# A four-layer graph kernel on one NeuronCore: all issue times of its 64 pipelined graphs laid out anew

## The chip, the cores and the metric

The kernel runs on one core of a Trainium2 chip. The core has five instruction streams that run beside each other: TensorE (PE in the profile, with its weight loads as PEld), VectorE (DVE), ScalarE (ACT), GpSimd (POOL) and SyncE (SP), which here only issues DMAs. Each stream takes its instructions strictly in the order in which the program holds them, and waits at an instruction until the inputs and the buffers of that instruction are free. The metric is the device time of one execution in microseconds; the median of several executions counts.

## The reference

64 graphs of 256 nodes with 512 features go through four layers. Every layer normalizes, applies a graph operation and adds the result to its input:

```python
# x: (64, 256, 512), adj: (64, 256, 256)
for layer in (L0, L1, L2, L3):
    h = jnp.maximum(_layernorm(x, axis=-1), 0.0)
    x = x + layer(h, adj, ...)

# L0: w = softmax_nodes(sum_m((q k^T / 8) * adj)),  out = w * (h Wv^T)
# L1: attention of 8 heads: leaky_relu(e_self + e_neigh), masked by adj, softmax, times features
# L2: per head tanh(adj * (Xc Xp^T)) Xp, with Xc = Xp C^T
# L3: w = softmax_nodes(sum_d(q * (adj k)) / sqrt(512)),  out = w * (h Wv)
```

The four layers of a graph depend on each other; the 64 graphs don't.

## The kernel before

**One graph is a list of 150 steps.** The function `graph(b)` builds them as closures under short names. A step issues a few instructions of one engine, or the DMAs of one move. By layer, with the lines of the profile:

- Every layer k begins with the same front: `st`k (row statistics, DVE, L690), `rs`k (DVE, L697), `pw`k (a power on POOL, L701), `sh`k (DVE, L706), `hn`k (the normalized rows, ACT, L713), `sq`k (a transpose of 32x32 blocks, DVE, L645), `sw`k (the blocks to DRAM, one DMA of 512 KB, L733), `ht`k (read back as turned rows, four DMAs of 128 KB, L650). The matmuls that need turned rows wait for `ht`k.
- Layer 0: `qk`, `qe`, `score0`, `s0v` (DVE, L829), `pv00`, `pv01` (values, L639), `softp0`, `softv0` (L756), `softa0`, `softw0` (L768, L769), `add0` (DVE, L775).
- Layer 1: `fa`, `fb` (features, L639), `fae`, `fbe` (DVE, L854, L855, L865), `send`, `er`, `enes` (two rows per head through DRAM and to all partitions, L873 to L884), `max0` to `max3` (DVE, L896), `mxv`, `mxt`, `mr`, `mb` (the row maxima by the same way, L906 to L926), and for each pair of heads p `ea`p (ACT, L935), `eg`p (POOL, L942), `eb`p (DVE, L948), `ex`p (ACT, L954), `po`p (PE, L966), `eh`p (POOL, L975); `su`, `oe`, `se`, `sp`, `sr`; `sqo`, `swo`, `or` (the way through DRAM again: L783, L733, L796), `oa0`, `oa1` (POOL, L1032, L1034).
- Layer 2: `xp`, `xe` (L639, L1052), `sqx`, `swx`, `xpt` (L645, L733, L650), `xc`, `ps`, `tv` (DVE, L1129), `ta`, `py`, `ye` (ACT, L1120), `sqy`, `swy`, `yr` (L783, L733, L796), and the sum with the input in two halves: `yv` (DVE, L1149) and `yg` (POOL, L1149).
- Layer 3: `am`, `agg`, `ga`, `z` (L639), `zv` (L1189), `softp3` to `softw3`, `pv30`, `pv31`, `add3`, `store`.

**The order is written out by hand, as times.** The table `TIMES` gives every step of a graph a time after the graph's beginning; graph b begins at b times `PERIOD`. `Plan.sequence` sorts all steps of all 64 graphs by these times, and `Plan.run` issues them in this order, with a dependency that keeps each engine's instructions in it. The times themselves reach the chip in no other way: only the order that they give to each engine counts. With a table of 283 us and a period of 59, about five graphs are under way at once. The first six graphs, the last five and the loads of the weights have tables of their own (`FIRST`, `LAST`, `WEIGHTS`).

**Buffers** are taken from a pool when a step is traced, the one that was given back longest ago first: 8 PSUM banks, 5 of `xt`, 4 of `pair`, 3 of `ht`, 3 of `all`, 2 each of `hn`, `sq`, `cols`, `half` and others. A step that takes a buffer waits for the last user of that buffer.

All DMAs are issued by SP, 20 steps per graph, in the one order. A step such as `ht1` waits on SP until its `sw1` has landed, and all DMAs behind it in SP's order wait too.

Of the kernel before, what the change touches and what calls it, by code (L numbers as in the profile page):

```python
# [18 lines left out]
KC = D // P  # L19
# [16 lines left out]
PERIOD = 59.0  # L36
TIMES = {
    "load": 0.000, "st0": 8.598, "at": 14.291, "rs0": 17.770, "pw0": 18.151, "sh0": 19.827, "hn0": 20.197,
    "sq0": 22.027, "neg": 23.076, "sw0": 23.619, "ht0": 26.810, "negt": 33.560, "qk0": 36.920, "qk1": 37.838,
    "qe0": 38.562, "qe1": 39.097, "score0": 39.117, "s0v": 42.489, "softp0": 45.404, "softv0": 48.091,  # L40
    "softa0": 48.731, "pv00": 49.189, "softw0": 52.829, "pv01": 53.476, "add0": 56.587, "st1": 58.282,
    "rs1": 60.040, "pw1": 60.420, "sh1": 61.401, "hn1": 61.771, "sq1": 63.601, "sw1": 65.193, "ht1": 68.384,
    "fa1": 73.209, "fa0": 75.198, "fae0": 77.504, "fae1": 78.257, "send": 79.376, "er": 79.818, "enes": 83.628,
    "max0": 93.041, "ea0": 93.130, "ea1": 95.760, "max2": 97.616, "fb0": 97.757, "max1": 97.783, "max3": 99.552,
    "mxv": 102.131, "mxt": 103.746, "ea2": 104.173, "mr": 104.189, "eg1": 105.093, "mb": 107.595, "ea3": 108.549,
    "eg0": 108.704, "eb0": 112.651, "eb1": 113.945, "ex0": 114.332, "eg2": 115.240, "ex1": 115.461, "eh1": 117.705,
    "fb1": 118.902, "fbe0": 119.237, "eg3": 120.587, "fbe1": 121.996, "po0": 122.625, "po1": 123.961,
    "eb2": 124.009, "ex2": 125.487, "eb3": 125.789, "eh0": 126.598, "ex3": 126.782, "po2": 127.022, "oe0": 127.910,
    "su0": 128.127, "po3": 128.638, "eh3": 128.740, "oe1": 129.974, "eh2": 130.055, "sqo": 130.841, "su1": 131.698,
    "se": 132.525, "swo": 132.976, "or": 132.996, "sp": 136.188, "sr": 138.013, "oa0": 139.860, "oa1": 142.480,  # L50
    "st2": 145.314, "rs2": 147.072, "pw2": 147.452, "sh2": 148.433, "hn2": 148.803, "sq2": 150.633, "sw2": 152.225,
    "ht2": 155.416, "xp0": 159.864, "xp1": 163.649, "xe0": 166.754, "xe1": 167.673, "sqx": 168.592, "swx": 171.012,
    "xpt": 174.204, "xc": 179.698, "xcv": 181.830, "ps0": 183.981, "tv0": 187.172, "xca": 187.563, "ps1": 188.658,
    "ta0": 189.627, "tv3": 192.016, "tv1": 193.393, "tv2": 197.635, "ta1": 198.812, "ta3": 200.645, "ta2": 201.909,
    "py0": 202.513, "ye0": 202.533, "py1": 204.554, "ye1": 206.911, "sqy": 207.777, "swy": 211.577, "am": 212.932,
    "yr": 217.212, "yv": 221.001, "yg": 221.746, "st3": 223.517, "rs3": 225.557, "pw3": 225.938, "sh3": 230.347,
    "hn3": 230.717, "agg1": 233.270, "agg0": 235.086, "sq3": 238.587, "sw3": 240.179, "ga0": 241.452,
    "ga1": 242.287, "ht3": 248.180, "z0": 254.433, "z1": 257.973, "zv0": 258.289, "zv1": 261.830,
    "softp3": 265.594, "pv31": 265.839, "softv3": 268.089, "softa3": 268.742, "pv30": 269.380, "softw3": 274.098,
    "add3": 280.909, "store": 282.605,  # L60
# [3 lines left out]
    "wn0": 288.300, "w12": 288.700, "mt0": 289.000, "wa": 289.100, "mv0": 289.200, "sa2": 289.300, "w11": 289.400,  # L64
    "wqk": 289.500, "w10": 289.900, "sa0": 290.600, "sa1": 290.700, "wv0": 290.800, "mk": 291.000, "b1": 291.500,
    "wn1": 291.600, "w20": 292.600, "w22": 292.800, "w13": 293.200, "b2": 294.000, "mm0": 294.100, "wn2": 294.200,
    "mt1": 294.300, "mv1": 294.400, "mkp": 294.500, "mt2": 294.600, "sa3": 295.000, "mm1": 295.300, "wn3": 295.700,
    "mv2": 295.800, "w21": 296.100, "mm2": 296.300, "mt3": 298.000, "mv3": 298.200, "mm3": 298.700, "mkv": 298.800,
    "c2": 298.900, "wv3": 299.200, "w23": 301.000, "ma": 302.600, "room": 303.100,
# [367 lines left out]
def tile_four_gnn_layers(ctx: ExitStack, tc: tile.TileContext, x, adj, nodemask,  # L437
# [6 lines left out]
    nc = tc.nc  # L444
# [790 lines left out]
```

## Time and profile before

| | |
|---|---|
| time before, median of 5 runs | 3896.66 us (3888.99 to 3902.02) |
| the profiled execution: device time | 3896.66 us |
| its span, first to last instruction | 3894.9 us |
| DVE busy | 3055.0 us (78%), 7449 instructions |
| ACT busy | 1872.2 us (48%), 3653 instructions |
| POOL busy | 1531.3 us (39%), 1229 instructions |
| DMA | 784.71 MB, mean 201 GB/s |
| granted TensorE clock, mean | 0.990 |
| SP's longest kind of wait: L650 for `sq_d` to land | 485.2 us, 247 times |

The profiled execution took exactly the median's time. A busy share is an average over the whole span. What the kernel repeats is a round: in every round each engine does each of the 150 steps once, for five different graphs. So the profile is read by the round: from a step of one graph to the same step of the next.

### The profile page before, as it was taken

The page shows a single profiled execution, that of the slowest core. Times are in us where ns is not written, and L with a number is a line of the kernel's source. Part 1 is how long each engine was busy: PE and PEld are TensorE (multiplying, and loading weights), DVE is VectorE, ACT ScalarE, POOL GpSimd, SP SyncE. Part 2 cuts the span into 40 slices and gives each one's busy share as a digit, 9 for nine tenths or more (in the row PEclk, how much of TensorE's full clock was granted, in tenths as well). Part 3 has the DMA queues.
Part 4 walks back from the last instruction along what each step waited for, and adds up shares of the span by engine and source line. Part 5 has one row for each costly group of instructions (what it writes and reads, how often), then busy time and mean ns, then how long its engine had stood idle before and what let it go on. Part 6 is the DMA issues. An engine that isn't in the chain of part 4 may idle for free.

```text
span 3894.9 us, 52870 instructions
## 1 busy us (share of the span) xinstructions
PE 3680.3 (94%) x16322; PEld 2126.9 (55%) x16322; DVE 3055.0 (78%) x7449; ACT 1872.2 (48%) x3653; POOL 1531.3 (39%) x1229
## 2 busy tenths in 40 slices
PE   6789999999999999999999999999999999999889
PEld 4445555555555555555555555555555555555544
DVE  5778788888788788788787788787788788787784
ACT  2444545544544545444544545544544544554442
POOL 1434344344344344344344344344344344343341
PEclk9899999999999999999999999999999999999999
DMA  7565666666666666666666666666666666666553
GB/s 199 168 201 190 203 200 212 218 197 217 211 206 215 206 212 208 202 208 208 206 195 214 207 197 214 215 199 216 206 201 216 211 196 216 210 197 198 184 176 103
DMA packets 967435, 784.71 MB, mean 201 GB/s; under 512 B 788913, under 2 KB 859121, under 8 KB 942577
## 3 DMA queue, kind: packets, MB, share of 16 engines
q1 hardware_dynamic: 967152, 781.34, 63.9%
q8 instruction: 130, 2.13, 0.2%
q14 instruction: 153, 1.25, 0.1%
HBM read 511.12 MB, written 270.01 MB: 201 GB/s over the span
## 4 chain that ended last, share of the span: by engine, by line
PE 48%; DVE 19%; DMA 17%; SPq 8%; issue 5%; POOL 2%; ACT 1%; DVEq 0%; ACTq 0%; POOLq 0%
PE bank L639 35%; DVE sq L645 7%; DMA ht<-sq_d 6%; DMA sq_d<-sq 5%; SPq L650 5%; PE bank L1111 5%; PE bank L966 2%; DVE pair L948 2%; PE bank L1097 2%; DMA blocks<-in_adj_dram 2%; DMA hn<-sq_d 2%; DVE stats L690 2%; DVE shift L706 1%; DVE xt L775 1%; DVE junk L896 1%
## 5 line engine op out<-in xcount | busy, mean ns | idle before, releaser
L639 PE MATMUL bank<-w_s,ht 128*128 128x256 f32 (+2 forms) x3072 | 968.9, 463 | 86.2 <-DMA ht<-sq_d 76.1
L639 PE MATMUL bank<-wv_s,ht 128*128 128x512 f32 x2048 | 907.5, 595 | 0.0
L639 PEld LDWEIGHTS bank<-w_s,ht 128*128 128x128 f32 x3072 | 588.9, 198 | 388.6 <-issue 295.3
L713 ACT ACTIVATE hn<-xt,shift,rstd 128x512 f32<-128x512 f32 x512 | 388.7, 807 | 830.5 <-DVE shift L706 772.5
L942 POOL TENSOR_TENSOR pair<-pair,negt 128x1024 f32<-128x1024 f32 x256 | 603.0, 2367 | 112.7 <-ACT pair L935 112.7
L639 PEld LDWEIGHTS bank<-wv_s,ht 128*128 128x128 f32 x2048 | 397.6, 197 | 445.9 <-issue 443.7
L975 POOL TENSOR_TENSOR half<-pair 128x512 f32<-128x512 f32 x256 | 330.8, 1304 | 594.7 <-PE bank L989 326.8
L896 DVE CUSTOM_DVE_ANT_0 junk<-all,adj 128x256 f32<-128x256 f32 x1024 | 467.3, 456 | 31.4 <-issue 0.2
L639 PE MATMUL bank<-m_s,ht 128*128 128x512 f32 x1024 | 454.3, 595 | 8.3 <-DMA ht<-sq_d 6.6
L935 ACT ACTIVATE pair<-all,ec 128x256 f32<-128x256 f32 x1024 | 433.4, 497 | 10.5 <-DMA all<-er_d 10.4
L1149 POOL TENSOR_TENSOR xt<-xt,hn 128x512 f32<-128x512 f32 x64 | 111.9, 1749 | 816.2 <-DMA hn<-sq_d 816.2
L690 DVE BATCH_NORM_STATS2 stats<-xt 128x6 f32<-128x512 f32 x512 | 332.5, 682 | 92.5 <-POOL xt L1034 84.8
L701 POOL TENSOR_TENSOR rstd<-rstd,power 128x2 f32<-128x2 f32 x256 | 180.5, 705 | 406.6 <-DVE rstd L697 390.9
L645 DVE STREAM_TRANSPOSE sq<-hn 128x512 f32<-128x512 f32 x512 | 332.1, 687 | 5.1 <-ACT hn L713 4.9
L1129 DVE TENSOR_TENSOR pair<-bank,at 128x512 f32<-128x512 f32 x512 | 317.3, 670 | 12.3 <-PE bank L1097 12.1
L966 PE MATMUL bank<-pair,feats 128*64 128x256 f32 x2048 | 270.9, 399 | 59.2 <-ACT pair L954 58.6
L954 ACT ACTIVATE pair<-pair 128x1024 f32<-128x1024 f32 x256 | 264.0, 1050 | 118.3 <-DVE pair L948 111.3
L639 PEld LDWEIGHTS bank<-m_s,ht 128*128 128x128 f32 x1024 | 196.9, 197 | 220.6 <-issue 215.1
L948 DVE TENSOR_TENSOR pair<-pair,all 128x1024 f32<-128x1024 f32 x256 | 303.1, 1222 | 16.1 <-DMA all<-m_d 16.0
L1032 POOL TENSOR_TENSOR hn<-hn,rs 128x256 f32<-128x256 f32 x256 | 152.1, 616 | 393.3 <-DMA hn<-sq_d 280.5
L761 ACT ACTIVATE bank<-bank,nmax 128x256 f32<-128x256 f32 x128 | 56.9, 444 | 501.7 <-DVE nmax L756 501.7
L1136 ACT ACTIVATE pair<-pair 128x512 f32<-128x512 f32 x512 | 285.8, 617 | 16.5 <-DVE pair L1129 16.4
(83 smaller groups left out, 4545.0 us busy)
## 6 DMA issues: line engine op xcount, KB each, us to landing
sq_d<-sq SPq DMA_DIRECT2D x448, 512.0 KB
ht<-sq_d SPq DMA_DIRECT2D x1024, 128.0 KB
all<-er_d SPq DMA_DIRECT2D x128, 1024.0 KB
all<-m_d SPq DMA_DIRECT2D x64, 1024.0 KB
hn<-sq_d SPq DMA_DIRECT2D x512, 128.0 KB
xt<-in_x_dram SPq DMA_DIRECT2D x64, 512.0 KB
xpt<-sq_d SPq DMA_DIRECT2D x256, 128.0 KB
out_dram<-xt SPq DMA_DIRECT2D x64, 512.0 KB
```

Of the source, the lines that this page charges most:

```text
L639: nc.tensor.matmul(p, chunk(ht[:, k], c), w[:, k], start=(k == 0), stop=(k == KC - 1))
L645: nc.vector.transpose(sq.rearrange("p (r k i c) -> p c k r i", r=4, k=KC, c=NC)[:, c], t[:, c])
L690: nc.vector.bn_stats(stats[:, c, :], g["xt"][:, c, :])
L713: nc.scalar.activation(hn[:, c, :], g["xt"][:, c, :], AF.Relu, bias=st["shift"][:, c:c + 1], scale=st["rstd"][:, c:c + 1])
L896: nc.vector.tensor_tensor_reduce(junk, g["en"][:, h, :], g["adj"][:, c, :], 1.0, -BIG, OP.add, OP.max, g["mx"][:, c, h:h + 1])
L935: nc.scalar.activation(e[:, s, j, :], g["es"][:, h, :], AF.Prelu, bias=st["ec"][:, j, H + h:H + h + 1], alpha=0.2)
L942: nc.gpsimd.tensor_tensor(e, e, g["negt"][:, None].to_broadcast([P, 2, NC, N]), OP.add)
L948: nc.vector.tensor_tensor(e, e, g["m"][:, 2 * p:2 * p + 2, None, :].to_broadcast([P, 2, NC, N]), OP.subtract)
L966: nc.tensor.matmul(po[s * U:(s + 1) * U, p % 2, :], feats[:, j, h * U:(h + 1) * U], e[:, s, j, :], start=(j == 0), stop=(j == NC - 1))
L975: nc.gpsimd.tensor_tensor(g.take("half", name=f"h{p}"), e[:, :, 0, :], e[:, :, 1, :], OP.add)
L1129: nc.vector.tensor_tensor(th[:, s], g[f"ps{p}{s}"].rearrange("p (m n) -> p m n", m=NC), g["at"], OP.mult)
L1136: nc.scalar.activation(g[f"th{p}"][:, s], g[f"th{p}"][:, s], AF.Tanh)
```

## The change

`PERIOD`, `TIMES`, `WEIGHTS`, `FIRST` and `LAST` get new values. The steps, their instructions, their buffers and the way in which the order is issued stay. In the setup, the two banks of each of the four weight transposes get names of their own (`wt0` becomes `wt00` to `wt03`), so that the transposes of one part can stand in the order before the copies of the part before it.

```diff
-PERIOD = 59.0
+PERIOD = 57.0
 TIMES = {
-    "load": 0.000, "st0": 8.598, "at": 14.291, "rs0": 17.770, "pw0": 18.151, "sh0": 19.827, "hn0": 20.197,
-    "sq0": 22.027, "neg": 23.076, "sw0": 23.619, "ht0": 26.810, "negt": 33.560, "qk0": 36.920, "qk1": 37.838,
-    "qe0": 38.562, "qe1": 39.097, "score0": 39.117, "s0v": 42.489, "softp0": 45.404, "softv0": 48.091,
-    "softa0": 48.731, "pv00": 49.189, "softw0": 52.829, "pv01": 53.476, "add0": 56.587, "st1": 58.282,
-    "rs1": 60.040, "pw1": 60.420, "sh1": 61.401, "hn1": 61.771, "sq1": 63.601, "sw1": 65.193, "ht1": 68.384,
-    "fa1": 73.209, "fa0": 75.198, "fae0": 77.504, "fae1": 78.257, "send": 79.376, "er": 79.818, "enes": 83.628,
-    "max0": 93.041, "ea0": 93.130, "ea1": 95.760, "max2": 97.616, "fb0": 97.757, "max1": 97.783, "max3": 99.552,
-    "mxv": 102.131, "mxt": 103.746, "ea2": 104.173, "mr": 104.189, "eg1": 105.093, "mb": 107.595, "ea3": 108.549,
-    "eg0": 108.704, "eb0": 112.651, "eb1": 113.945, "ex0": 114.332, "eg2": 115.240, "ex1": 115.461, "eh1": 117.705,
-    "fb1": 118.902, "fbe0": 119.237, "eg3": 120.587, "fbe1": 121.996, "po0": 122.625, "po1": 123.961,
-    "eb2": 124.009, "ex2": 125.487, "eb3": 125.789, "eh0": 126.598, "ex3": 126.782, "po2": 127.022, "oe0": 127.910,
-    "su0": 128.127, "po3": 128.638, "eh3": 128.740, "oe1": 129.974, "eh2": 130.055, "sqo": 130.841, "su1": 131.698,
-    "se": 132.525, "swo": 132.976, "or": 132.996, "sp": 136.188, "sr": 138.013, "oa0": 139.860, "oa1": 142.480,
-    "st2": 145.314, "rs2": 147.072, "pw2": 147.452, "sh2": 148.433, "hn2": 148.803, "sq2": 150.633, "sw2": 152.225,
-    "ht2": 155.416, "xp0": 159.864, "xp1": 163.649, "xe0": 166.754, "xe1": 167.673, "sqx": 168.592, "swx": 171.012,
-    "xpt": 174.204, "xc": 179.698, "xcv": 181.830, "ps0": 183.981, "tv0": 187.172, "xca": 187.563, "ps1": 188.658,
-    "ta0": 189.627, "tv3": 192.016, "tv1": 193.393, "tv2": 197.635, "ta1": 198.812, "ta3": 200.645, "ta2": 201.909,
-    "py0": 202.513, "ye0": 202.533, "py1": 204.554, "ye1": 206.911, "sqy": 207.777, "swy": 211.577, "am": 212.932,
-    "yr": 217.212, "yv": 221.001, "yg": 221.746, "st3": 223.517, "rs3": 225.557, "pw3": 225.938, "sh3": 230.347,
-    "hn3": 230.717, "agg1": 233.270, "agg0": 235.086, "sq3": 238.587, "sw3": 240.179, "ga0": 241.452,
-    "ga1": 242.287, "ht3": 248.180, "z0": 254.433, "z1": 257.973, "zv0": 258.289, "zv1": 261.830,
-    "softp3": 265.594, "pv31": 265.839, "softv3": 268.089, "softa3": 268.742, "pv30": 269.380, "softw3": 274.098,
-    "add3": 280.909, "store": 282.605,
+    "load": 0.000, "st0": 0.020, "at": 0.040, "rs0": 0.041, "pw0": 1.190, "sh0": 5.411, "hn0": 9.143, "neg": 9.823,
+    "sq0": 13.810, "sw0": 13.830, "negt": 20.103, "ht0": 20.147, "qk1": 25.359, "qk0": 25.505, "qe0": 25.525,
+    "qe1": 31.036, "score0": 31.056, "pv00": 31.112, "s0v": 32.547, "softp0": 32.567, "softv0": 34.836,
+    "softa0": 34.856, "softw0": 35.790, "pv01": 40.387, "add0": 43.272, "st1": 43.292, "rs1": 44.358,
+    "pw1": 46.056, "sh1": 46.076, "hn1": 49.648, "sq1": 51.260, "sw1": 58.135, "ht1": 60.945, "fa0": 60.965,
+    "fa1": 62.580, "fae0": 69.453, "fae1": 70.533, "send": 70.553, "er": 70.573, "enes": 71.911, "ea0": 77.990,
+    "max0": 78.143, "ea2": 80.895, "max3": 81.818, "max1": 83.190, "fb0": 85.227, "max2": 87.498, "mxv": 87.518,
+    "mxt": 87.571, "eg0": 94.088, "mr": 94.796, "fbe0": 95.764, "ea1": 97.749, "eg1": 97.769, "mb": 98.261,
+    "fb1": 99.101, "eb0": 100.193, "eg2": 100.883, "ea3": 101.474, "ex0": 101.699, "fbe1": 102.120, "eb2": 103.469,
+    "po0": 105.075, "eg3": 106.212, "ex2": 106.927, "eb1": 108.590, "eb3": 108.607, "ex1": 108.610, "ex3": 108.627,
+    "eh1": 108.630, "po2": 110.140, "eh0": 110.672, "po1": 111.849, "po3": 112.568, "oe0": 112.800, "oe1": 112.820,
+    "su0": 113.279, "eh2": 114.993, "sqo": 115.048, "swo": 119.512, "eh3": 121.483, "su1": 121.503, "or": 123.062,
+    "se": 124.801, "sp": 126.234, "sr": 128.731, "oa0": 128.751, "oa1": 133.174, "st2": 133.194, "rs2": 133.214,
+    "pw2": 133.973, "sh2": 134.814, "hn2": 134.834, "sq2": 138.696, "sw2": 138.716, "ht2": 150.552, "xp0": 152.412,
+    "xp1": 153.173, "xe0": 156.059, "xe1": 156.636, "sqx": 156.656, "swx": 160.517, "xpt": 163.712, "xc": 163.798,
+    "xcv": 169.374, "ps0": 170.351, "tv1": 172.876, "ta1": 172.896, "xca": 176.954, "tv0": 177.175, "ps1": 182.074,
+    "ta0": 184.632, "py0": 184.652, "tv2": 186.879, "ta2": 186.899, "tv3": 187.157, "am": 187.177, "ta3": 189.350,
+    "ye0": 190.185, "py1": 191.616, "ye1": 191.636, "sqy": 191.656, "swy": 191.676, "yr": 195.931, "yg": 201.775,
+    "yv": 203.676, "st3": 204.853, "rs3": 205.841, "pw3": 205.861, "sh3": 206.511, "hn3": 209.985, "agg0": 213.022,
+    "sq3": 213.434, "sw3": 214.903, "ga0": 217.074, "agg1": 217.232, "ht3": 218.661, "z0": 220.014, "ga1": 228.472,
+    "zv0": 240.578, "z1": 240.673, "zv1": 244.494, "softp3": 244.514, "softv3": 244.534, "pv30": 249.208,
+    "pv31": 250.464, "softa3": 253.023, "softw3": 256.850, "add3": 262.864, "store": 272.661,
 }
...
@@ -594,7 +592,7 @@
             @step(f"mt{e}")
             def _():
                 for s in range(2):
-                    pt = g.take("bank", name=f"wt{s}")
+                    pt = g.take("bank", name=f"wt{s}{e}")
                     for k in range(KC):
                         nc.tensor.transpose(pt[:, k * P:(k + 1) * P], st[f"wn{e}"][:, s, k], ident)
 
@@ -602,10 +600,10 @@
             def _():
                 st["w_t"] = w_t = once.tile([P, 2, D], F32, name="w_t", bufs=1)
                 nc.vector.tensor_copy(w_t[:, 0, :].rearrange("p (k d r) -> p k d r", k=KC, r=4),
-                                      g["wt0"].rearrange("p (k r d) -> p k d r", k=KC, r=4))
-                nc.vector.tensor_copy(w_t[:, 1, :], g["wt1"])
-                g.done("wt0")
-                g.done("wt1")
+                                      g[f"wt0{e}"].rearrange("p (k r d) -> p k d r", k=KC, r=4))
+                nc.vector.tensor_copy(w_t[:, 1, :], g[f"wt1{e}"])
+                g.done(f"wt0{e}")
+                g.done(f"wt1{e}")
 
             @step(f"mm{e}")
             def _():
```

The tables `WEIGHTS`, `FIRST` and `LAST`, left out here, are replaced in the same way. At the start, the loads of graphs 0 and 1 now both stand ahead of the first weights on SP (before: that of graph 0 alone), and graph 1's steps come earlier among those of graphs 0 and 2.

What the table of the repeating round means for each engine, from the first `fa` on, follows from sorting it. The number behind a step says how many rounds earlier its graph was loaded; `-1` is the next graph:

```
before
PE: fa1.1 fa0.1 sp.2 z0.4 z1.4 py0.3 py1.3 softp3.4 pv31.4 pv30.4 qk0.0 qk1.0 fb0.1 score0.0 xp0.2 softp0.0 xp1.2
  pv00.0 pv01.0 agg1.3 agg0.3 fb1.1 xc.2 po0.1 po1.1 ps0.2 po2.1 su0.1 po3.1 ps1.2 su1.1
DVE: fae0.1 fae1.1 sh0.0 sr.2 send.1 tv2.3 sq0.0 zv0.4 zv1.4 st2.2 rs2.2 sh2.2 sqy.3 softv3.4 sq2.2 max0.1 softw3.4
  max2.1 max1.1 max3.1 s0v.0 mxv.1 yv.3 mxt.1 add3.4 st3.3 softv0.0 rs3.3 xe0.2 xe1.2 sqx.2 softw0.0 sh3.3 eb0.1 eb1.1
  add0.0 st1.0 rs1.0 fbe0.1 sh1.0 sq3.3 fbe1.1 sq1.0 eb2.1 eb3.1 st0.-1 tv0.2 sqo.1 at.-1 tv3.2 tv1.2 rs0.-1
SP: swo.2 or.2 er.1 sw0.0 enes.1 ht0.0 sw2.2 swy.3 ht2.2 yr.3 mr.1 store.4 mb.1 swx.2 xpt.2 load.-1 sw3.3 sw1.0 ht1.0
  ht3.3
POOL: oa0.2 oa1.2 pw2.2 yg.3 eg1.1 pw3.3 eg0.1 eg2.1 eh1.1 pw1.0 eg3.1 eh0.1 eh3.1 eh2.1 pw0.-1
ACT: hn0.0 ta1.3 neg.0 ta3.3 ta2.3 ye0.3 ye1.3 hn2.2 softa3.4 negt.0 ea0.1 am.3 ea1.1 qe0.0 qe1.0 ea2.1 softa0.0 ea3.1
  hn3.3 ex0.1 ex1.1 hn1.0 xcv.2 ga0.3 ga1.3 ex2.1 ex3.1 oe0.1 xca.2 oe1.1 ta0.2 se.1
after
PE: fa0.1 fa1.1 su1.2 ps1.3 sp.2 z1.4 py0.3 softp3.4 py1.3 pv30.4 pv31.4 qk1.0 qk0.0 fb0.1 score0.0 pv00.0 softp0.0
  xp0.2 xp1.2 pv01.0 agg0.3 fb1.1 agg1.3 po0.1 z0.3 xc.2 po2.1 po1.1 po3.1 su0.1 ps0.2
DVE: tv1.3 sh0.0 tv0.3 fae0.1 zv0.4 fae1.1 send.1 sq0.0 sr.2 tv2.3 tv3.3 zv1.4 softv3.4 st2.2 rs2.2 sqy.3 sh2.2 max0.1
  sq2.2 max3.1 max1.1 softw3.4 max2.1 mxv.1 mxt.1 s0v.0 yv.3 st3.3 softv0.0 rs3.3 add3.4 sh3.3 softw0.0 fbe0.1 xe0.2
  sq3.3 xe1.2 sqx.2 eb0.1 add0.0 st1.0 rs1.0 fbe1.1 sh1.0 eb2.1 sq1.0 eb1.1 eb3.1 st0.-1 at.-1 rs0.-1 sqo.1
SP: swo.2 or.2 er.1 sw0.0 enes.1 ht0.0 swy.3 sw2.2 yr.3 ht2.2 mr.1 mb.1 sw3.3 store.4 swx.2 ht3.3 xpt.2 load.-1 sw1.0
  ht1.0
POOL: oa0.2 oa1.2 pw2.2 yg.3 pw3.3 eg0.1 eg1.1 eg2.1 pw1.0 eg3.1 eh1.1 eh0.1 eh2.1 pw0.-1 eh3.1
ACT: hn0.0 neg.0 se.2 ta0.3 ta2.3 am.3 ta3.3 ye0.3 negt.0 ye1.3 hn2.2 ea0.1 ea2.1 softa3.4 qe0.0 qe1.0 softa0.0 hn3.3
  ea1.1 ea3.1 ex0.1 ga0.3 hn1.0 ex2.1 ex1.1 ex3.1 xcv.2 oe0.1 oe1.1 ga1.3 ta1.2 xca.2
```

On POOL, `pw3` now stands directly ahead of `eg0`, `eg1` and `eg2`; `pw1` and `eg3` follow them, with `eh1` no longer between. On SP, `load` stands directly ahead of `sw1`, `yr` directly ahead of `ht2`, and `ht3` moves from behind `ht1` to ahead of `xpt`. On DVE, `yv` and `st3` stand directly behind `s0v`; `eb0` is the only `eb` ahead of `add0`; `su1` and `ps1` on PE stand behind `fa1`.

## The prediction

> **What bounds the kernel now.** First the busy time by stretches of the span (start:end, length, then busy time and count of each engine). I cut it where graph 8's `z0` begins (698 us) and where that of graph 48 begins (3032.4): 40 whole rounds.
>
> ```profile
> core 0: us, PE busy (x) PEld busy (x) DVE busy (x) ACT busy (x) POOL busy (x), PEclk, DMA share, GB/s
> 0.00:350.00 350.00, 276.21 (x1169) 164.66 (x1170) 248.57 (x580) 136.49 (x261) 120.04 (x106) 0.94 0.62 187
> ...
> 698.00:3032.40 2334.40, 2261.75 (x10163) 1314.11 (x10162) 1872.30 (x4640) 1164.55 (x2280) 950.96 (x760) 1.00 0.66 208
> ...
> 3540.00:3895.00 355.00, 315.56 (x1314) 171.42 (x1312) 250.44 (x535) 145.96 (x277) 114.43 (x91) 0.96 0.51 158
> ```
>
> A round takes 2334.4 / 40 = 58.36 us and holds 2261.75 / 40 = 56.54 us of PE work. So the repeating part can give at most 1.8 us a round. PE idles 73.8 us in the first 350 and 39.4 in the last 355. Who ends PE's waits in those 40 rounds, from the view of waits:
>
> ```profile
> PE bank L639 <- DMA ht<-sq_d: 44.8, 52, 2.0
> PE bank L966 <- ACT pair L954: 18.9, 33, 1.0
> ```
>
> PE waits for turned rows and for `ex`, a fraction of a microsecond each. That is the mark of a loop through several engines that is a little longer than PE's own work. I look for it in the timeline of the round that begins with `fa1` at 3028.40 (three answers: PE, DVE, SP):
>
> ```profile
> 3028.40 3.91 PE L639 MATMUL bank<-w_s,ht 128*128 128x272 f32 x16
> ...
> 3086.82 3.91 PE L639 MATMUL bank<-w_s,ht 128*128 128x272 f32 x16 [0.20 <-DMA ht<-sq_d]
> ```
> ```profile
> 3054.86 0.23 DVE L829 SCALAR_TENSOR_TENSOR bank<-bank,qk 128x64 f32<-128x64 f32 x1 [0.26 <-PE bank L821]
> ...
> 3057.73 0.69 DVE L1149 TENSOR_TENSOR xt<-xt,hn 128x512 f32<-128x512 f32 x1 [1.15 <-DMA hn<-sq_d]
> ...
> 3070.29 1.40 DVE L775 SCALAR_TENSOR_TENSOR xt<-bank,w,xt 128x512 f32<-128x512 f32 x2
> ...
> 3074.11 2.30 DVE L706 SCALAR_TENSOR_TENSOR shift<-mv,rstd 128x2 f32<-128x2 f32 x1 [0.49 <-POOL rstd L701]
> ...
> 3077.87 1.27 DVE L645 STREAM_TRANSPOSE sq<-hn 128x512 f32<-128x512 f32 x2
> ```
> ```profile
> 3077.66 1.86 SPq L733 DMA_DIRECT2D sq_d<-sq  x2
> 3081.85 5.24 SPq L650 DMA_DIRECT2D ht<-sq_d  x8
> ```
>
> The loop has three legs: `fa` to `s0v` 26.46 us; `s0v` to `add0` 15.43; `add0` by `st1`, `rs1`, `pw1`, `sh1`, `hn1`, `sq1`, `sw1`, `ht1` to the next `fa` 16.53. Sum 58.42.
>
> **The port.** `sh1` (L706) takes 2.30 us here, for two columns. POOL's `eg3` (L942) runs at the same time, and `sh1` ends as it does:
>
> ```profile
> 3074.05 2.35 POOL L942 TENSOR_TENSOR pair<-pair,negt 128x1024 f32<-128x1024 f32 x1
> ```
>
> Where three `eg` follow each other (129.25 to 136.81), `max` (L896, 0.42 alone) reads 2.44 each time:
>
> ```profile
> 129.67 2.44 DVE L896 CUSTOM_DVE_ANT_0 junk<-all,adj 128x256 f32<-128x256 f32 x1
> ...
> 132.16 2.45 DVE L896 CUSTOM_DVE_ANT_0 junk<-all,adj 128x256 f32<-128x256 f32 x1
> ```
>
> So a DVE instruction of this kind waits for the POOL instruction under way, but gets in before the next one. [...]
>
> **The change, part by part.** No instruction is added or removed; what moves is who waits behind whom. I lay the three legs again in the new order, with durations from rows; a following DVE instruction begins about 0.08 us before the end of the one ahead (3070.29 + 1.40 against `st1` at 3071.61), so I use start-to-start steps.
>
> *Leg 1.* PE: `fa0`, `fa1` 3.91 (row above), `su1` 0.57, `ps1` 1.94, `sp` 0.23, `z1` 3.44, `py0`, `py1` 3.60, `softp3` 0.36 = 14.05. Then `ye1` 0.6 with its wait (L1120 597 ns), `sqy` 1.17, `sh2` 0.1; DVE arrives at `max0` at 16.0. `enes` must be there: `send` is done at 4.85 (two `fa`, `fae1` 0.6, `send` 0.25), `er` to `enes` takes about 3.2, `enes` to `max0` took at least 8.1 before, but DVE never idled for it there, so this is an upper end: 16.2. Covered to within 0.2. Then four `max` of 1.87, `sq2` 1.21, `softw3` 0.14, `mxv` and `mxt` 1.13 = 9.96: `s0v` could begin at 26.0. But `yr` now issues as soon as `sw2` has, not behind `ht2`; `y` lands 4.7 later (3052.92 to 3057.63), at about 24.3, while `max2` runs (23.0 to 24.9). POOL is idle there and `yg` takes the port for 1.78 us. `s0v` begins at 27.8. PE comes to `softp0` at 28.8, so PE does not wait. `yr`'s move costs leg 1 1.3 us against before; bounds 0 (`y` lands behind `mxv`) and 1.78.
>
> *Leg 2.* `s0v` 0.54, `yv` 0.61, `st3` 1.45, `softv0` 0.31: `rs3` at 2.9 after `s0v` begins. Before, DVE idled 1.15 for `y`, and `eb1` stood ahead of `add0` (1.14): both are gone. `pw3` begins 0.25 later and takes 0.66, and `eg0` stands directly behind it: `sh3` is ready at 4.5 and is held until `eg0` ends at 6.2, a new loss of 1.7. From there, `hn3` 1.45, `ea1` 1.75, `eg1` 2.35 end at 5.6 after. DVE meanwhile: `softw0` 0.15, `fbe0` 0.31, `xe0` 0.61, wait for `hn3` to about 1.45, `sq3` 1.21, `xe1` 0.61, `sqx` 2.07 = 5.3. `eb0` asks 0.3 us before `eg1` ends and gets in ahead of `eg2`: 5.6, plus 1.14. `add0` begins at 6.2 + 6.75 = 12.95 instead of 15.43. Bounds of `eb0`'s wait: 0 and 2.35 (one `eg`); I take 0.3 by the rows of `max`.
>
> *Leg 3.* The same steps, `eg3` again behind `pw1`, so `sh1` again 2.30: 16.45 (the row's 16.53 less its 0.08 of PE). New is that `load` (six issues, 3.1 us: 3071.82 to 3074.86 in the SP order before) is directly ahead of `sw1`. `swx`, `ht3`, `xpt` and `load` end on SP about 6.9 us after `add0` begins, `sw1` comes at 8.9: it does not wait on SP, but its 512 KB queue behind the load's 1 MB, issued 2 us earlier instead of 4. `sw1` to `ht1` was 2.65. Bounds 0 and 1.2 more; I take 0.4. `ht3` to `z0`, `xpt` to `xc` and `po3`'s `ex3` I find within 0.3 us of PE's arrival: they lie under the 0.7 us that PE then idles ahead of `fa0`. If that idle went, they would cost up to 0.3. The front `st0`, `at` of the next graph come about 7 us behind `load`: hidden by `sq1`, `eb1`, `eb3`.
>
> Sum: 27.8 + 12.95 + 16.45 + 0.4 = **57.6 us a round against 58.36**. Graphs 8 to 58 make 50 such rounds: 50 x 0.76 = 38 us less.
>
> *Ends.* The first eight and the last five graphs are laid out anew too, with the same instructions. Ahead of the first weights stands one more `load` (3.1 us of SP, covered by graph 0's own front before `sw0`). PE idles 113 us at the two ends; a quarter of it either way, 28 us, is my bound for them, and 0 my value, as no row favours a side. The renamed banks cost nothing: the transposes (L599) are 6.0 us of PE in all. Time: 3896.7 - 38 = **3859 us** (the profiled execution is the median run).
>
> **Rivals.**
>
> *PE alone.* `y` lands outside `max2` and no step loses the port: the loop falls to 55.9 and PE's 56.54 rules, 56.7 with small waits. 50 x 1.66 = 83: 3814. For it: PE's work is that short. Against: the landing falls in the middle of `max2`.
>
> *Nothing gained.* `sw1` pays the full 1.2 us behind `load`: 58.4 a round, 3897. For it: SP has waited up to 7.0 us for an `sq_d`. Against: the load's bytes are mostly through by then.
>
> *Slower: `eb0` loses to `eg2`.* `eg1` ends just before `eb0` asks, `eg2` begins, `eb0` waits 2.35, `add0` begins 2.05 later and so does everything behind it: 59.65 a round, 50 x 1.29 = 64, 3961. It decides from 0.3 us: if `sqx` ends more than that later, or `eg1` that much earlier, than laid out. For it: a margin of 0.3 at the end of nine steps, and nothing in the new order keeps `eg2` off. Against: the rows that show DVE getting in.
>
> *The change doesn't do what it says*: longer reads in the times alter the chip's work only through order, so with the same order nothing would move; the order does differ in all five streams.
>
> **How the numbers follow.** Forecast 0.52 (57.2 to 58.0 a round: 3840 to 3885 with small ends), PE alone 0.12, nothing gained 0.10, slower 0.26. A measurement of this kernel tells 0.2%, 8 us, from no change. Faster: 0.52 + 0.12 = 0.64; same 0.10; slower 0.26. Range for 8 in 10: 3805 (PE alone, ends 9 better) to 3945 (the slower case with the ends 16 better or with `eb0` losing in three rounds of four); about 0.04 lies below and 0.16 above. The forecast's own range is 3840 to 3885.
>
> **What would show it.** `fa` to `fa` at 57.2 to 58.0. `L1149` of POOL inside `L896`, one of which reads about 2.2 us. All `L706` of layers 1 and 3 long, so its mean above the 650 ns of before. `L948` with no more than 0.5 us of waiting in the first of each round; 3.3 us there would be the slower rival. `sw1` to `ht1` 3.0; 3.9 would be nothing gained. PE's waits for `ht` before `fa0`, none before `xp0`. Wrong altogether if the ends move more than 28 us, or if DVE idles for `enes` ahead of `max0`.

## The result and the profile after

The changed kernel takes 3896.99 us (median, 3889.05 to 3902.29) against 3896.57 us for the kernel before, measured beside it. The ratio is 0.9999 with a 95% interval of 0.9993 to 1.0005: no change, where 3859 us was forecast. The profiled execution has a span of 3899.9 us, 5.0 more than before.

First the busy time by stretches, cut at the same times as before (start:end, length, then busy time and count of each engine):

```profile
core 0: us, PE busy (x) PEld busy (x) DVE busy (x) ACT busy (x) POOL busy (x), PEclk, DMA share, GB/s
0.00:350.00 350.00, 285.95 (x1225) 167.09 (x1226) 266.30 (x622) 147.49 (x282) 125.40 (x109) 0.93 0.65 195
...
698.00:3032.40 2334.40, 2277.85 (x10056) 1291.15 (x10054) 2009.90 (x4616) 1168.67 (x2261) 926.16 (x751) 1.00 0.67 206
```

In the long stretch DVE is busy 2009.90 us instead of 1872.30, with 24 instructions fewer. So the same instructions became longer. The groups of costly instructions say which: `eb` (L946, before L948) has a mean of 1588 ns instead of 1222, `sh` (L704, before L706) 1052 instead of 650. The rows, two of before and two of after (count | busy us, mean ns of one | idle us before):

```profile
L948 DVE TENSOR_TENSOR pair<-pair,all 128x1024 f32<-128x1024 f32 x256 | 303.1, 1222 | 16.1 <-DMA all<-m_d 16.0
L706 DVE SCALAR_TENSOR_TENSOR shift<-mv,rstd 128x2 f32<-128x2 f32 x256 | 166.4, 650 | 83.5 <-POOL rstd L701 83.2
L946 DVE TENSOR_TENSOR pair<-pair,all 128x1024 f32<-128x1024 f32 x256 | 400.8, 1588 | 13.6 <-DMA all<-m_d 13.6
L704 DVE SCALAR_TENSOR_TENSOR shift<-mv,rstd 128x2 f32<-128x2 f32 x256 | 269.3, 1052 | 41.3 <-POOL rstd L699 41.3
```

Over 256 of each that is 94 + 103 = 197 us, all but some 5 us of DVE's growth over the whole span (3055.0 to 3256.6 us). What a DVE instruction loses beside a POOL one is not shown as idle time before it; it stands inside its own duration: `eb0` takes 3.21 us at 1541.66 below and 1.21 at 3018.47, with no idle time before either. The recorded texts call this wait the port; the traces show when the instructions begin and end, not what the two engines share.

A typical round, from the timelines of DVE, POOL and SP (start, duration, engine, line; a bracket is idle time before, with what ended it):

```profile
1538.97 0.69 DVE L1050 TENSOR_TENSOR xp<-bank,b_bc 128x512 f32<-128x512 f32 x1 [0.62 <-PE bank L637]
1539.58 2.15 DVE L643 STREAM_TRANSPOSE sq<-xp 128x512 f32<-128x512 f32 x2
1541.66 3.21 DVE L946 TENSOR_TENSOR pair<-pair,all 128x1024 f32<-128x1024 f32 x1
1544.79 1.40 DVE L773 SCALAR_TENSOR_TENSOR xt<-bank,w,xt 128x512 f32<-128x512 f32 x2
```
```profile
1539.10 4.69 POOL L940 TENSOR_TENSOR pair<-pair,negt 128x1024 f32<-128x1024 f32 x2 [3.31 <-ACT pair L933]
```
```profile
1548.83 1.91 SPq L664 DMA_DIRECT2D blocks<-in_adj_dram  x4
1553.33 0.34 SPq L731 DMA_DIRECT2D sq_d<-sq  x1
1556.01 2.54 SPq L648 DMA_DIRECT2D ht<-sq_d  x4
```

POOL's two `eg`, `eg1` and `eg2`, run from 1539.10 to 1543.79; the record of `eg2` alone begins at 1541.43. `eb0` asks at 1541.66, 0.24 us later by the single records, and ends at 1544.87, 1.08 us after `eg2`. `add0` follows at 1544.79. In 46 of the 50 rounds from graph 8 to graph 58 `eb0` is 0.11 to 0.34 us too late and takes some 3.1 us. In the other four it asks 0.03 to 0.14 us ahead of `eg2`'s start and gets in. Here is one of these four, again DVE, POOL and SP:

```profile
3018.47 1.21 DVE L946 TENSOR_TENSOR pair<-pair,all 128x1024 f32<-128x1024 f32 x1
```
```profile
3016.18 5.75 POOL L940 TENSOR_TENSOR pair<-pair,negt 128x1024 f32<-128x1024 f32 x2 [3.30 <-ACT pair L933]
```
```profile
3025.69 1.91 SPq L664 DMA_DIRECT2D blocks<-in_adj_dram  x4
3028.10 0.34 SPq L731 DMA_DIRECT2D sq_d<-sq  x1
3031.58 2.54 SPq L648 DMA_DIRECT2D ht<-sq_d  x4
```

Now POOL pays (5.75 for two `eg` instead of 4.69), and a second thing shows: `sw1` (L731) stands directly behind the load's last issue, and `ht1` follows it after 3.48 us instead of 2.68. That round took 57.25 us, not the 56.4 that 2 us less would give.

The round against what was laid (medians over the 50 rounds, start to start):

| | before | laid | after |
|---|---|---|---|
| `fa` to `s0v` | 26.5 | 27.8 | 27.2 |
| `s0v` to `add0` | 14.7 | 12.95 | 15.18 |
| `add0` to the next `fa` | 16.5 | 16.85 | 16.05 |
| mean round | 58.37 (median 58.17) | 57.6 | 58.71 (median 58.42) |

The mean is above the median because ten rounds take 59 to 61.2 us (the kernel before has eleven of 59 to 60.8). In seven of the ten, `sw1` to `ht1` or `ht1` to `fa` is long. The other three, those of graphs 31, 38 and 41, each follow directly on the worst of the seven: there the granted TensorE clock is 0.5 for 3.4 us as the round begins, and legs 1 and 2 take 1.6 to 1.8 us longer. The spans add up: graph 8's first `fa` comes at 509.4 us instead of 520.6 (11.2 less), 50 rounds cost 2935.4 instead of 2918.4 (17.0 more), the rest 455.1 instead of 455.9.

### The profile page after: what moved, and what is told of

It reads as the page before. It is cut to its first block, busy times and chain, and to the rows that moved or that the text cites. A ratio compares the mean times of both kernels' runs of the same rounds, so it can differ in the third digit from the quotient of the medians.

```text
span 3899.9 us, 53075 instructions
## 1 busy us (share of the span) xinstructions
PE 3720.8 (95%) x16322; PEld 2107.8 (54%) x16322; DVE 3256.6 (84%) x7449; ACT 1893.1 (49%) x3653; POOL 1507.9 (39%) x1229
## 4 chain that ended last, share of the span: by engine, by line
PE 40%; DVE 27%; issue 10%; POOL 9%; ACT 6%; DMA 5%; SPq 3%; DVEq 0%; ACTq 0%; POOLq 0%
PE bank L637 23%; DVE junk L894 8%; POOL pair L940 6%; PE bank L1109 6%; PE bank L1095 5%; DVE sq L643 3%; DVE pair L946 3%; DVE shift L704 2%; POOL half L973 2%; ACT pair L933 2%; DMA ht<-sq_d 2%; ACT hn L711 2%; DVE xt L773 2%; SPq L648 2%; PE bank L987 2%
## 5 line engine op out<-in xcount | busy, mean ns | idle before, releaser
L637 PE MATMUL bank<-wv_s,ht 128*128 128x512 f32 x2048 | 926.6, 600 | 15.2 <-DMA ht<-sq_d 11.9
L637 PE MATMUL bank<-m_s,ht 128*128 128x512 f32 x1024 | 466.3, 599 | 3.4 <-DMA ht<-sq_d 3.4
L933 ACT ACTIVATE pair<-all,ec 128x256 f32<-128x256 f32 x1024 | 422.1, 494 | 15.1 <-DMA all<-er_d 14.7
L1134 ACT ACTIVATE pair<-pair 128x512 f32<-128x512 f32 x512 | 299.5, 625 | 264.6 <-DVE pair L1127 264.5
L946 DVE TENSOR_TENSOR pair<-pair,all 128x1024 f32<-128x1024 f32 x256 | 400.8, 1588 | 13.6 <-DMA all<-m_d 13.6
L1147 POOL TENSOR_TENSOR xt<-xt,hn 128x512 f32<-128x512 f32 x64 | 82.5, 1288 | 616.0 <-DMA hn<-sq_d 616.0
L704 DVE SCALAR_TENSOR_TENSOR shift<-mv,rstd 128x2 f32<-128x2 f32 x256 | 269.3, 1052 | 41.3 <-POOL rstd L699 41.3
```

What stands on the lines that cost most here:

```text
L637: nc.tensor.matmul(p, chunk(ht[:, k], c), w[:, k], start=(k == 0), stop=(k == KC - 1))
L704: nc.vector.scalar_tensor_tensor(st["shift"], st["mv"][:, :, 0], -1.0, st["rstd"], op0=OP.mult, op1=OP.mult)
L933: nc.scalar.activation(e[:, s, j, :], g["es"][:, h, :], AF.Prelu, bias=st["ec"][:, j, H + h:H + h + 1], alpha=0.2)
L946: nc.vector.tensor_tensor(e, e, g["m"][:, 2 * p:2 * p + 2, None, :].to_broadcast([P, 2, NC, N]), OP.subtract)
L1134: nc.scalar.activation(g[f"th{p}"][:, s], g[f"th{p}"][:, s], AF.Tanh)
```

## The experiments

The theory after the result had two parts: `eb0` comes 0.3 us too late to go ahead of `eg2`, which costs leg 2 two microseconds; and behind that hides a price of the `load` ahead of `sw1`, which shows only where `eb0` is early. The rival: either one alone is the whole story. In the kernels below, keys not shown are those of the changed kernel (or of the kernel before, where that is said). Legs and single durations are medians over the 50 rounds, rounds are means unless it says median. Ratios are to the kernel before, timed on the same chip.

**e1_eb0: `eb0` ahead of `xe1`.**

```diff
-"eb0": 100.193
+"eb0": 99.500
```

> The changed kernel with one step moved on DVE: eb0 directly ahead of xe1, where DVE idled for xp1, instead of behind sqx. In the changed kernel eb0 takes 3.1 us in a round because eg2 holds the port, and the round is 58.7 us in the mean. Theory (port, then queue): eb0 falls to 1.2 and the leg from s0v to add0 from 15.2 to 12.9 us, but sw1 then follows the load's last issues by about 2 us instead of 4.4, its write lands 1 to 2 us later, and the round only falls to 57.7 to 58.3: 3850 to 3880 us. Rival 1 (port alone): sw1 to ht1 stays at 2.7 and the round falls to 56.8: about 3800. Rival 2 (TensorE or VectorE work sets the round, the port does not matter): 3890 to 3900.

Measured: 3927.14 us, ratio 1.0052 (1.0038 to 1.0066), above all three ranges expected. From the timelines of DVE and SP:

```profile
3039.89 1.17 DVE L946 TENSOR_TENSOR pair<-pair,all 128x1024 f32<-128x1024 f32 x1
...
3050.83 1.29 DVE L643 STREAM_TRANSPOSE sq<-hn 128x512 f32<-128x512 f32 x2
```
```profile
3047.09 2.60 SPq L648 DMA_DIRECT2D xpt<-sq_d  x4
3049.73 0.62 SPq L659 DMA_DIRECT2D xt<-in_x_dram  x1
3050.39 0.43 SPq L660 DMA_DIRECT2D adj<-in_adj_dram  x1
3050.87 1.91 SPq L664 DMA_DIRECT2D blocks<-in_adj_dram  x4
3052.88 0.39 SPq L731 DMA_DIRECT2D sq_d<-sq  x1
3056.74 2.55 SPq L648 DMA_DIRECT2D ht<-sq_d  x4
```

`eb0` takes 1.18 and leg 2 falls from 15.18 to 12.49 us: the first part of the theory holds. But `sq1` is done at 3052.12 here, and SP issues the load until 3052.78; `sw1` follows only then. Over the rounds `sq1` to `sw1` grows from 1.3 to 2.0 us (start to start), `sw1` to `ht1` from 2.7 to 4.5, the two together from 4.0 to 6.7, and leg 3 from 16.05 to 18.89. What leg 2 gained, 2.7, leg 3 gave back with 2.8.

That makes no change, yet the mean round is 59.25 us, and the kernel is slower. The rest is the clock. PE's gap ahead of `fa` is now 1.9 us in the median round (0.1 in the changed kernel), and in 16 of the 50 rounds the granted clock falls to 0.5 for 3.4 us behind a gap of 1.9 to 4.2. Here are two rows of the view by stretches, in a dip and right behind it (columns as in the first fence, the clock third from the end), then PE's `fa0` and `fa1` in this round of e1, and in an undisturbed round of the changed kernel:

```profile
2408.47:2411.88 3.41, 3.41 (x9) 2.60 (x8) 0.47 (x3) 1.72 (x3) 0.00 (x0) 0.50 0.44 111
2411.88:2425.00 13.12, 13.12 (x78) 7.33 (x78) 8.36 (x23) 6.40 (x12) 5.58 (x7) 1.00 0.69 241
```
```profile
2407.89 5.60 PE L637 MATMUL bank<-w_s,ht 128*128 128x272 f32 x16 [2.25 <-DMA ht<-sq_d]
```
```profile
3036.44 3.91 PE L637 MATMUL bank<-w_s,ht 128*128 128x272 f32 x16 [0.47 <-issue]
```

The same matmuls take 1.7 us longer. The changed kernel has three such dips in its 50 rounds; the 13 more of e1 are 22 of the 27 us by which its 50 rounds are longer. The 34 rounds without a dip have a median of 58.44 us, against 58.39 for the 47 such rounds of the changed kernel: `eb0` ahead of `xe1` alone is worth nothing.

**e2_eg2: `eg2` behind `pw1` on POOL,** so that nothing follows `eg1` when `eb0` asks.

```diff
-"eg2": 100.883
+"eg2": 103.200
```

> The changed kernel with one step moved on POOL: eg2 behind pw1, so that no eg can run when eb0 comes; DVE's order is untouched. Theory (port, then queue): eb0 falls from 3.1 to 1.2 us, sh1 still reads 2.3 (it now waits for eg2), and sw1 lands later behind the load; round 57.6 to 58.3, 3850 to 3880 us. Rival 1 (port alone): round about 56.9, 3805. Rival 2 (the long eb0 is a wait for its DMA, not for the port): eb0 stays long, 3890 to 3900.

Measured: 3914.22 us, ratio 1.0019 (1.0010 to 1.0027), above all ranges expected. DVE and POOL:

```profile
3024.59 1.23 DVE L946 TENSOR_TENSOR pair<-pair,all 128x1024 f32<-128x1024 f32 x1
...
3029.57 2.30 DVE L704 SCALAR_TENSOR_TENSOR shift<-mv,rstd 128x2 f32<-128x2 f32 x1 [0.39 <-POOL rstd L699]
3031.88 3.36 DVE L946 TENSOR_TENSOR pair<-pair,all 128x1024 f32<-128x1024 f32 x1
```
```profile
3029.50 4.66 POOL L940 TENSOR_TENSOR pair<-pair,negt 128x1024 f32<-128x1024 f32 x2
```

`eb0` is free and leg 2 13.2, but now `eg2` and `eg3` stand behind `pw1` together: `sh1` pays for the first and `eb2`, which stands ahead of `sq1`, for the second. Leg 3 is 18.3, the round 58.87. `sw1` to `ht1` stays at 2.7, so the load plays no part in this loss: it moved from `eb0` to two other DVE steps of the same loop.

**e3_load: the load behind `ht1` instead of ahead of `sw1`,** with the front of layer 0 moved to follow it, `eb0` as in the change. **e4_both: the same and `eb0` ahead of `xe1`.**

```diff
-"load": 0.000, "st0": 0.020, "at": 0.040, "rs0": 0.041, "pw0": 1.190, "sh0": 5.411, "hn0": 9.143, "neg": 9.823,
-"sq0": 13.810, "sw0": 13.830
+"load": 4.000, "st0": 13.600, "at": 13.620, "rs0": 13.610, "pw0": 13.650, "sh0": 14.740, "hn0": 14.760, "neg": 20.200,
+"sq0": 16.200, "sw0": 16.210
```

> The changed kernel with the load moved behind ht1 on SP, and the first steps of the loaded graph (st0, rs0, pw0, at, sh0, hn0, sq0, sw0, neg) moved later on their engines to match; eb0 stays as it is. Theory (port, then queue): sw1 to ht1 stays near 2.7 us in all rounds (the changed kernel has 3.0 to 4.8 in about a third of graphs 28 to 43), eb0 still takes 3.1; a round 58.3 to 58.6, 3880 to 3895 us. Rival 3 (the load ahead of sw1 alone made the loss): round below 57.5, 3840 or less.

> Both edits at once: eb0 ahead of xe1, and the load behind ht1 with the first steps of its graph later. Theory (port, then queue): eb0 1.2, sw1 to ht1 2.7, the loop falls to about 56.4 and TensorE's own work of 56.5 sets the round at 56.7 to 57.2: 3805 to 3830 us, more than the sum of what either edit gives alone. Rival 2 (TensorE or VectorE work sets the round already): 3880 to 3900. Rival 4 (another wait stands just behind, such as ht0 for qk1 or the row maxima): 57.5 to 58.2, 3845 to 3880.

Measured: 4199.17 us, ratio 1.0746 (1.0730 to 1.0762), and 4114.82, 1.0522 (1.0503 to 1.0541): both far from what was expected. In e3_load `sw1` to `ht1` is 2.67, but `sw0` now stands behind `enes`. Its SP and PE:

```profile
3057.12 0.34 SPq L881 DMA_DIRECT2D all<-er_d  x1
3057.56 0.38 SPq L882 DMA_DIRECT2D all<-er_d  x1
3058.04 0.38 SPq L731 DMA_DIRECT2D sq_d<-sq  x1
```
```profile
3010.57 2.15 PE L637 MATMUL bank<-wqk_s,ht 128*128 128x128 f32 x16 [3.12 <-DMA ht<-sq_d]
```

`enes` is two broadcasts of 1 MB each; `sw0`'s 512 KB behind them land late (`sw0` to `ht0` is 8.7 us, 3.0 in the change), and PE waits at `qk1`, 4.0 us in the median round. This edit made a new wait of its own and so did not answer the question about the load's place. The pair still says something: with `eb0` early the kernel is 84 us faster than without, so where no load stands ahead of `sw1`, `eb0`'s place is worth 1.7 us a round (64.29 against 62.56), in a kernel with this other wait in it.

**e7_split: the load taken apart.** `adj` and `blocks` (five issues, 512 KB) go where SP is idle, between `mb` and `sw3`; `xt` alone (one issue, 512 KB) stays. `eb0` late as in the change. **e8_eb0_split: the same and `eb0` ahead of `xe1`. e9_eb0_split2: as e8, with `xt` too moved, ahead of `xpt`** (time -8.0 instead of 0.0, for the graphs 12 to 55). The core of the edit:

```diff
-"load": 0.000
+"load": -15.500
...
+            steps += [(b * PERIOD + (0.0 if times is TIMES else times["load"] - 0.001), b, "loadx")]
...
         @step("load")
         def _():
-            nc.sync.dma_start(g.take("xt"), x[b].rearrange("(p c) d -> p c d", c=NC))
...
+        @step("loadx")
+        def _():
+            nc.sync.dma_start(g.take("xt"), x[b].rearrange("(p c) d -> p c d", c=NC))
```

> The changed kernel, only with the load taken apart: adj and blocks (five issues, 512 KB) are issued between mb and sw3, where SP is idle for some 5 us, and the xt issue (512 KB) alone stays ahead of sw1. eb0 still stands behind xe1. Theory (eb0's wait for eg2 sets the round, and the load behind it costs nothing as long as eb0 is late): nothing gained, eb0 still 3.1 us, leg 2 still near 15.2, a round of 58.3 to 58.7, 3890 to 3900 us. Rival (the load ahead of sw1 costs leg 3 something already in the changed kernel): sw1 to ht1 falls below 2.7 us and the round to 57.9 or less, 3860 us.

> eb0 ahead of xe1 as in the first experiment, and the load taken apart: adj and blocks between mb and sw3, xt alone (one issue, 512 KB) ahead of sw1. Theory (eb0's port is worth some 2 us, and what ate it was SP still issuing the load when sq1 was done, plus sw1's write behind the load's 1 MB): sq1 to sw1 back to 1.3 us from 2.2, sw1 to ht1 between 2.7 and 3.5 us from 4.5, leg 3 between 16.3 and 17.2 from 18.9, leg 2 12.5 to 13.0; a round of 56.6 to 57.3, PE's gap ahead of fa0 below 0.5 us, 3795 to 3835 us. Rival (it isn't the load; a write that follows close on sqx, ht3 and xpt is slow by itself): sw1 to ht1 stays at 4 us or more, the round at 58.5 or more, 3890 us or more.

> As the run before, but in the repeating rounds the xt issue too stands earlier, between ht3 and xpt, so that nothing of the load is directly ahead of sw1. Theory: if the 512 KB of xt still cost sw1 something in the run before, sw1 to ht1 falls here to 2.6 to 2.8 us and leg 3 to 16.3; in exchange xpt is issued 0.4 us later and lands behind 512 KB, up to 1.5 us, and PE then waits that long at xc, which follows within 0.3 us now: a round between 56.6 and 58, 3795 to 3865 us. Rival (xt ahead of sw1 costs nothing): the run before is the faster of the two by what xpt loses.

Measured: 3891.89 us, 3828.15 and 3829.39; ratios 0.9964 (0.9951 to 0.9976), 0.9798 (0.9782 to 0.9814) and 0.9802 (0.9786 to 0.9818).

e7: the median round stays at 58.36 and `eb0` at 3.13, as expected; the mean round falls to 58.36 with fewer long rounds (4 over 59 us instead of 10) and no dip of the clock in the 50, and the 0.36% fit that. e8 is the case that decides. Its DVE, its SP, and its 40-odd middle rounds in the view by stretches (columns as in the first fence):

```profile
3005.42 1.19 DVE L950 TENSOR_TENSOR pair<-pair,all 128x1024 f32<-128x1024 f32 x1
...
3016.42 1.29 DVE L644 STREAM_TRANSPOSE sq<-hn 128x512 f32<-128x512 f32 x2
```
```profile
2999.51 0.79 SPq L660 DMA_DIRECT2D adj<-in_adj_dram  x1
3000.35 1.90 SPq L664 DMA_DIRECT2D blocks<-in_adj_dram  x4
...
3015.43 0.62 SPq L669 DMA_DIRECT2D xt<-in_x_dram  x1
3017.74 0.33 SPq L735 DMA_DIRECT2D sq_d<-sq  x1
3020.75 2.56 SPq L649 DMA_DIRECT2D ht<-sq_d  x4
```
```profile
690.00:2990.00 2300.00, 2292.36 (x10274) 1317.87 (x10273) 1949.70 (x4686) 1196.02 (x2308) 950.27 (x770) 1.00 0.70 213
```

`sq1` is done at 3017.71 and `sw1` leaves at 3017.74. `sq1` to `sw1` is 1.3 again, `sw1` to `ht1` 3.28, leg 2 12.46, leg 3 17.08, the median round 56.74 (mean 56.98), and no round has a dip of the clock. The four kernels together, by their median rounds without a dip: 58.39 for the change, 58.44 with `eb0` early, 58.36 with the load apart, 56.74 with both. PE is busy 2292.36 of 2300 us, 99.7%: here PE itself is the bound. e9 shows the rest of the queue's price: with `xt` 5 us ahead, `sw1` to `ht1` falls to 2.85, but `xpt` lands later, PE waits for it at `xc` (0.22 us in the mean; the bound of 1.5 was an estimate) and the median round is 57.06. Both times lie where they were expected and can't be told apart; e9's leg 3 is 17.3, not the 16.3 expected.

**e11_before_eb1: one part of the change alone, on the kernel before. e12_before_eb1_split: the same with the load taken apart.**

```diff
-"eb1": 113.945, "ex1": 115.461, "eh1": 117.705, "po1": 123.961
+"eb1": 123.000, "ex1": 123.100, "eh1": 123.300, "po1": 126.000
```

> One part of the change alone, on the kernel before: eb1 moves on DVE from ahead of add0 to behind sq1, with what hangs on it (ex1 behind hn1 on ACT, eh1 behind eg3 on POOL, po1 behind ps0 on PE). Everything else, the load too, as before. Theory (the loop of three legs sets the round, and eb1 is 1.14 us of leg 2): s0v to add0 falls from 14.7 to 13.6, sw1 comes 1.1 us closer behind the load (6.4 us becomes 5.3) and pays nothing or up to 0.5 us for it; a round of 57.2 to 57.8, 3840 to 3870 us. Rival (what is pushed behind sq1 is late for PE: eb1, eb2, eb3 in a row, and PE waits at po2 or su0): leg 2 falls as in the theory, but leg 3 grows by as much in PE's gaps at po2, su0 or po3; a round of 58.2 or more, 3885 us or more.

> The run before with the load taken apart as in the two best kernels so far: adj and blocks in SP's idle stretch between mb and swx, xt alone behind xpt. Theory: if the load still costs sw3 and sw1 something, this is faster than the run before by what sw1 to ht1 (2.7 us in the kernel before) and ht1 to the next fa lose there, 0 to 0.5 us a round; 56.9 to 57.6 us a round, 3820 to 3860 us, so that two small edits of the old order come near the best of the new one (3828). Rival (the load is far enough from sw1 in the old order): the same as the run before within 8 us.

Measured: 3970.13 us, ratio 1.0160 (1.0145 to 1.0176), and 3967.73, 1.0155 (1.0141 to 1.0170). Leg 2 falls from 14.72 to 13.65 as both theories said, but leg 3 grows from 16.47 to 19.20. PE, in e11:

```profile
3026.59 1.08 PE L966 MATMUL bank<-pair,feats 128*64 128x256 f32 x8 [1.00 <-ACT pair L954]
3028.51 1.08 PE L966 MATMUL bank<-pair,feats 128*64 128x256 f32 x8 [0.83 <-ACT pair L954]
3029.82 0.64 PE L989 MATMUL bank<-half,ones 128*32 128x256 f32 x8 [0.22 <-POOL half L975]
```

`po1`, `po2` and `su0` wait for the late `ex` and `eh`, 2.06 us in the mean round (0.75, 0.83, 0.48): the rival. In this order `eb1` stands early because PE needs it early. The changed kernel has `eb1` behind `sq1` too, with `z0` and `xc` between `po0` and the other `po` on PE; that these two give `ex` the time is likely, but no run takes them out. Taking the load apart is worth nothing here: PE's wait comes behind it.

## Why the prediction was wrong

**The step that failed** is the sentence in leg 2: "`eb0` asks 0.3 us before `eg1` ends and gets in ahead of `eg2`". Measured, in 46 of 50 rounds it asks 0.11 to 0.34 us after `eg2` has begun. Counted from `fa`, DVE's own time was right: `eb0` asks at 39.3 us after `fa0`, as laid. `eg1` ends at 39.1, and was laid at 39.6. Two terms made that. `yg` was laid to cost leg 1 1.78 us, its duration before; here it takes 1.27 and holds DVE for 1.0, so `s0v` and all that follows on DVE and POOL came 0.6 sooner. DVE then lost this 0.6 again, because `xe1` waits 0.6 us for PE's `xp1`, a wait that I had not laid. The chain to `eg1` by way of ACT and POOL (`hn3`, `ea1`, `eg1`) has no such wait and kept all but 0.1 of it. What I had read from the rows of `max`, that DVE gets in between two POOL instructions if it asks before the second begins, held for `eb0` in all 50 rounds: it takes 1.18 to 1.26 us in the four in which it asks first, 3.1 to 3.4 in the 46 others. What was wrong was to take 0.3 us of margin at the end of nine steps as decided.

**The rival "slower: `eb0` loses to `eg2`" named the wait, its place and its price** (2.05 us; measured about 2.0). Its time was too high, 59.65 against 58.42 for the median round, because leg 1 was 0.6 shorter than laid and leg 3 0.8.

**The term for the load, 0.4 of 0 to 1.2,** an estimate for which the prediction names no row, was mis-sized and is invisible in the result. In the changed kernel `add0` is so late that `sw1` follows the load's last four issues by 4.4 us, measured from their start, and pays nothing in the median round (2.70 against 2.69). With `eb0` in time, as the forecast had it, e1 shows 0.7 us of SP still issuing and 1.8 us more to the landing, together 2.7 by the median of the sum: over twice the upper bound. I had the load's issues end 6.9 us after `add0` begins; in e1 they end at 9.1. So had the failed step come true, the forecast would still have been missed: 27.2 + 12.5 + 18.9 = 58.6, no better than the kernel before. The four early rounds of the changed kernel itself show part of it (`sw1` to `ht1` 3.5 to 4.4).

**The yardstick was off too.** The gain of 0.76 sets a sum of typical steps (57.6) against a mean round (58.36). The one round of the kernel before that the prediction read adds up to 58.42, with 15.43 in leg 2; the median of leg 2 over the 50 rounds is 14.72, and the medians of the three legs add up to 57.7. The mean round lies 0.7 above that sum (in the changed kernel 0.3), through rounds in which one leg is long. Measured alike, 57.6 against 57.7, the laid order was hardly better than the old one.

**What held.** `sh3` waits 1.7 us for `eg0` (measured 1.88 against 0.15 long) and `sh1` still takes 2.30. PE's wait ahead of `xp0` is gone (0.76 to 0). DVE does not idle for `enes` ahead of `max0`. The ends moved by 12 us, inside the 28 allowed. `yg` does hold DVE where `y` lands, but in most rounds it holds one of `mxv`'s four small instructions (some 1.2 us instead of 0.2, so 1.0), ahead of `mxt`, not `max2`; and this costs nothing at the end: in five rounds in which it holds them by 0.2 us at most, leg 1 is 26.2 to 26.4 and leg 2 15.9 to 16.1, and `add0` comes at the same time, since `eg2` sets it. "PE alone", forecast at 3814, is where e8 arrives (3828).

**What stays open.** Why `sw1` lands late in some rounds of the kernel before and of the changed one is not settled. In the changed kernel the rounds of graphs 30, 37 and 40 have 3.6 to 4.8 us from `sw1` to `ht1`, with the load as far ahead as in the others (4.4 to 4.5 us). In e7's profile the longest is 3.57, and its time is 0.24 to 0.49% below the kernel before, which speaks for the load all the same. Nor is it shown what sets off a dip of the clock: each of e1's came behind a gap of PE of 1.9 us or more, but other gaps of up to 2.3 us there had none behind them.

## What to carry to other kernels

Where the profile shows an instruction of one engine held by one of another, as `eb0` and `sh1` are here by `eg` (3.1 and 2.30 us instead of 1.2 and 0.15), an order is not "ahead" or "behind" by itself: lay both chains to the same instant, count every wait of each from PE too, and if the margin is a few tenths, price both outcomes and move the instruction until the margin is microseconds (here one step, `eb0` ahead of `xe1`). When a lost race is removed, ask at once which queue the work now arrives at sooner: here a write reached the DMA queue while a load was still being issued, and the gain of 2.7 us was paid back whole with 2.8. Neither edit alone brought more than 0.4%; both together brought 2.0%, down to PE's own work. And look at the clock before a longer mean is put down to a wait: compare the rounds at the full clock (in e1 the 13 more dips are 22 of the 27 us).

## What the runs showed of the hardware

- Beside an `eg` of POOL, `sh3` and `sh1`, with two columns per partition, take 1.88 and 2.30 us (0.15 alone), and `eb0`, with 1024, takes 3.1 (1.2 alone).
- In e1 `sw1`, a write of 512 KB that SP issues right behind a load of 1 MB, lands 1.8 us later (`sw1` to `ht1` 4.5 instead of 2.7). In e8, issued 2.3 us behind a load of 512 KB, it lands 0.6 later (3.28). In e3 `sw0`, 512 KB too, lands 5.7 later right behind two broadcasts of 1 MB (`sw0` to `ht0` 8.7 instead of 3.0).
- The mean granted clock is 0.988 in the changed kernel and 0.987 in e8, which is faster; it is 0.981 in e1, 0.967 in e3 and 0.961 in e4, and 0.988 in e11, where PE waits 2.06 us in the mean round. In e1 it falls to 0.5 for 3.4 us at a time, in 16 of 50 rounds, each time behind a gap of PE of 1.9 to 4.2 us; in the round shown `fa0` and `fa1` then take 5.60 us instead of 3.91.
